# A two-layer recurrent/MoE kernel: expert inputs scattered to their slots, and the recurrent states kept as rows in DRAM

## The chip, the core and the metric

The program runs on one core of one Trainium2 chip. The metric is the device time of one execution in microseconds; the lower, the better. The kernel before took 1542.63 us (median of 3 runs, 1536.48 to 1543.17).

Five engines work side by side, each on its own in-order list of instructions: TensorE (PE, with its weight loads shown apart as PEld), VectorE (DVE), ScalarE (ACT), GpSimd (POOL) and SyncE (SP), which here only issues DMAs. Plain DMAs are issued from SP's queue, indirect ones (rows picked by a list of indices in SBUF) from POOL's.

## What is computed

`x` has 4 sequences (batches b = 0..3) of 1024 tokens with 256 channels, in float32. Two layers, each of the form `x = x + s * silu(f)`, where `s` and `f` both start from the layer-normed `x`:

```
xn = layernorm(x)
s  = gru(xn)                       # layer 0: gated linear recurrence over the 1024 steps
g  = silu(moe0(xn))                # 16 experts, 4 of them per token, hidden width 128
x  = x + s * g
xn = layernorm(x)
s  = attention(xn)                 # layer 1: proj = cos(theta)*cos(xn), softmax(proj proj^T / 4) proj W_c^T + b_c
g  = silu(moe1(xn))                # shared expert of width 512 + 16 routed ones of width 64
x  = x + s * g
```

The router of layer 0 takes a sigmoid of 16 scores per token, keeps the best two of four groups of experts, then the best four experts, and weights their outputs by the normalised scores.

## The kernel before, in words

The Python program lists instructions in the order of the calls below; the framework then orders each engine's list itself, by readiness in its own model of time and with earlier calls first, and puts in the semaphore waits. So work of a later call may stand before that of an earlier one (in the trace the weight loads of L635 are issued ahead of the row stores of L216). Tiles with the same tag share a fixed number of buffers (`bufs`); a tile waits until one of them is free.

**Layer 0** treats the batches as two groups, (0,1) and (2,3), of 2048 tokens each. For a group:

- `prep0` (L619): loads x in halves of 512 tokens (`load_half`, L84, tag `x`, XB = 5 buffers), `norms` (L180) gives mean and variance, `norm_transposed` (L204) writes the normed rows (L212), stores them to DRAM as `rows_in` (L216) and transposes them on PE to `xnT`. `route` (L272) computes the scores (matmuls L283) and picks the experts on DVE. `places` (L329) gives each (token, choice) pair a slot: the slots of an expert fill tiles of 128, at most 80 tiles for a group. Then it builds, slot by slot, the **list** of which token sits there: 64 times (16 token tiles x 4 choices) POOL compares (`at`, L384), DVE compares (`who`, L386) and PE multiplies (L389).
- `gru` (L455): for each half and each 128 channels (four rounds per batch, 16 in all) four matmuls (L464), three ACT instructions (L473 to L475), four DVE ones (L476 to L480) and a scan along time (L482). The states `hT` stay in SBUF, channels on partitions (tag `big_a`, two buffers).
- `experts0` (L485): 40 pairs of slot tiles. Per pair, POOL fetches 2 x 128 token rows of `rows_in` by the list (L493), PE transposes them (L506), gate and up projections with the weights of that tile's expert (8 matmuls, L530), silu and product, transposes (L547), the down projection (L555), and one store to `rows_out` (L569).
- `gated0` (L584): per 128 tokens, POOL gathers the four expert rows of each token from `rows_out` (4 x L593), DVE weights and adds them (L599, L601), ACT takes silu of a half (L604), PE turns the states to rows (L611), DVE multiplies and adds (L613, L616), SP stores `x1` (L617).

The calls stand in this order (L631 to L644):

```
xnTs, *routed0 = prep0(0)          # then the weights w0 (L635)
hTs = [gru(t) for t in xnTs]
experts0(0, ...)
xnTs, *routed1 = prep0(1)
gated0(0, ...) for b = 0, 1
experts0(1, ...)
hTs = [gru(t) for t in xnTs]
gated0(1, ...) for b = 2, 3
```

**Layer 1** (L647 to L816) goes batch by batch: `prep1` (norm, cosine projection into tag `big_a`, values, routing), `attend` (scores L699, exp L707, sums L713), `ffn1` for each half (L442, L446, L768, L782). `prep1(b+1)` is called between the two halves of batch b.

Of the kernel before, what the change touches and what calls it, by code (L numbers as in the profile page):

```python
# [8 lines left out]
F32 = mybir.dt.float32  # L9
F16 = mybir.dt.float16  # L10
I32 = mybir.dt.int32
# [11 lines left out]
XB, RB, YB = 5, 3, 3  # L23
E, G = 16, 4
TOPK = 4
GROUPS0 = ((0, 1), (2, 3))
WE = 3 * D


def slot_tiles(n):  # L30


    most = n * TOPK // P + E - 1
    return most + most % 2
# [8 lines left out]
INV_2PI = 0.15915494309189535  # L43
MAGIC = 12582912.0
# [4 lines left out]
def two_layer_kernel(  # L49
# [97 lines left out]

    count1 = const.tile([P, P], F32, tag="count1", name="count1")
    nc.gpsimd.iota(count1, [[1, P]], base=1, channel_multiplier=0, allow_small_or_imprecise_dtypes=True)
# [4 lines left out]

    token = const.tile([P, NG], F32, tag="token", name="token")
    nc.gpsimd.iota(token, [[P, NG]], base=-NG * P // 2, channel_multiplier=1, allow_small_or_imprecise_dtypes=True)
# [4 lines left out]
    b2_sb = const.tile([P, 2 * KC], F32, tag="b2", name="b2_sb")  # L161
    nc.vector.tensor_scalar(b2_sb, bzh_sb, 2.0, None, ALU.mult)
# [41 lines left out]
    def norm_transposed(halves_, stat, keep=None):  # L204


        xnT = work.tile([P, KC, S], F32, tag="xnT", name="xnT", bufs=2)
        for q in range(NQ):
            xn = work.tile([P, NS, D], F32, tag="r", name="xn", bufs=RB)
            shift, rstd = stat[q]  # L210
            for s in range(NS):
                nc.scalar.activation(  # L212
                    xn[:, s, :], halves_[q][:, s, :], AF.Identity, bias=shift[:, s : s + 1], scale=rstd[:, s : s + 1]
                )
            if keep is not None:
                nc.sync.dma_start(  # L216
                    out=keep.rearrange("(c p) d -> p c d", p=P)[:, q * NS : (q + 1) * NS, :], in_=xn
                )
# [110 lines left out]
    def places(em, g):  # L329
# [32 lines left out]
        nc.vector.tensor_scalar(base, base, float(P), 1.0, ALU.mult, ALU.add)  # L362
# [10 lines left out]
        ptile = small.tile([P, nt, TOPK], F32, tag="ptile", name="ptile", bufs=1)  # L373
        nc.vector.tensor_scalar(ptile, top[:, :, 0:TOPK], 1.0 / P, -0.5 - 0.5 / P, ALU.mult, ALU.add)
        nc.vector.tensor_scalar(ptile, ptile, MAGIC, None, ALU.add)
        nc.vector.tensor_scalar(ptile, ptile, MAGIC, None, ALU.subtract)
        pin = small.tile([P, nt, TOPK], F32, tag="pin", name="pin", bufs=1)
        nc.vector.scalar_tensor_tensor(pin, ptile, -float(P), top[:, :, 0:TOPK], ALU.mult, ALU.add)  # L378

        lst = bank("tp", 2)  # L380
        for c in range(nt):
            for k in range(TOPK):
                at = small.tile([P, P], F16, tag="at", name="at", bufs=4)
                nc.gpsimd.tensor_scalar(at, count1, pin[:, c, k : k + 1], None, ALU.is_equal)  # L384
                who = small.tile([P, ns], F16, tag="who", name="who", bufs=4)
                nc.vector.tensor_scalar(  # L386
                    who, count0[:, 0:ns], ptile[:, c, k : k + 1], token[:, c : c + 1], ALU.is_equal, ALU.mult
                )
                nc.tensor.matmul(  # L389
                    lst[:, 0:ns],  # L390
                    lhsT=at,
                    rhs=who,
                    start=(c == 0 and k == 0),
                    stop=(c == nt - 1 and k == TOPK - 1),
                )
        who_in = small.tile([P, ns], I32, tag=f"who_in{g}", name="who_in", bufs=1)
        nc.vector.tensor_scalar(who_in, lst[:, 0:ns], float(NG * P // 2), None, ALU.add)


        nc.vector.tensor_scalar(who_in, who_in, float(nt * P - 1), None, ALU.min)  # L400
        slot = small.tile([P, nt, TOPK], I32, tag=f"slot_i{g}", name="slot_i", bufs=1)
        nc.vector.tensor_scalar(slot, top[:, :, 0:TOPK], -1.0, None, ALU.add)
# [3 lines left out]
        for t in range(0, ns, 32):  # L406
            n = min(32, ns - t)
            done = small.tile([1, n, E], F32, tag="hit", name="done", bufs=1)
# [8 lines left out]
        return who_in, slot, top, pos, of_tile  # L417

    def weights_by_slot(comb, top, pos, g):
# [3 lines left out]
        for i in range(0, nt, NT):  # L423
            ts = slice(i, i + NT)
            shape = [P, NT, TOPK, E]
            hit = small.tile(shape, F32, tag="hit", name="hit", bufs=1)
# [10 lines left out]
    def gate_up(wg, wu, xr):  # L437
# [11 lines left out]

    rows_in = [nc.dram_tensor(f"rows_in{g}", (len(s) * S, D), F32).ap() for g, s in enumerate(GROUPS0)]  # L450
    rows_out = [
        nc.dram_tensor(f"rows_out{g}", (slot_tiles(len(s) * S) * P, D), F32).ap() for g, s in enumerate(GROUPS0)
    ]

    def gru(xnT):  # L455

        hT = work.tile([P, KC, S], F32, tag="big_a", name="hT", bufs=2)
        for q in range(NQ):
            cols = slice(q * TB, (q + 1) * TB)
            for c in range(KC):  # L460
# [10 lines left out]
                w = work.tile([P, 4, TB], F32, tag="big_b", name="gru")  # L471
                tz, co, tg, rl = (w[:, i, :] for i in range(4))
                nc.scalar.activation(tz, pk, AF.Tanh, bias=hb_sb[:, c : c + 1], scale=0.5)  # L473
                nc.scalar.activation(tg, pp, AF.Tanh, bias=hb_sb[:, KC + c : KC + c + 1], scale=0.5)
                nc.scalar.activation(rl, pp, AF.Relu, bias=b2_sb[:, KC + c : KC + c + 1], scale=2.0)  # L475
# [6 lines left out]
                nc.vector.tensor_tensor_scan(hT[:, c, cols], co, tg, before, ALU.mult, ALU.add)  # L482
        return hT

    def experts0(g, who_in, of_tile):  # L485

        ns = who_in.shape[1]
        offsets = {}
# [387 lines left out]
```

## Time and profile before

| | |
|---|---|
| median of 3 runs | 1542.63 us |
| the profiled execution | 1543.79 us |
| its span, first to last instruction | 1542.1 us |
| busy in it: PE / DVE / POOL / ACT | 1290.4 / 562.3 / 374.3 / 351.8 us |
| mean granted TensorE clock | 0.892 |
| DMA moved | 100.93 MB |

The profiled execution's time is its span and 1.7 us around it. Busy time is the sum of an engine's instructions; it is an average over stages with different limits. By the first and last instructions of each stage in the trace, the span divides like this:

| from to (us) | stage | length |
|---|---|---|
| 0 to 121 | load, norms, routing and the list of group 0; GRU of batches 0, 1 | 121 |
| 121 to 268 | experts of group 0 | 147 |
| 268 to 405 | routing and list of group 1, gather and gate of group 0 | 137 |
| 405 to 553 | experts of group 1 (with a rest of the gating of group 0) | 148 |
| 553 to 660 | GRU of batches 2, 3, gather and gate of group 1 | 107 |
| 660 to 685 | what is left of `prep1(0)` | 25 |
| 685 to 1542 | attention and feed-forward of layer 1 | 857 |

### The profile page before, as it was taken

Reading aid. Unit: us, or ns where it says so; the run is one execution under the profiler, and the core shown is the slowest. Engines: PE = TensorE matmul, PEld = TensorE weight load, DVE = VectorE, ACT = ScalarE, POOL = GpSimd, SP = SyncE. Lnnn points to the kernel's source line nnn. Section 1 sums busy time; section 2 is a strip of 40 time slices with the busy share of each in tenths; the row PEclk is TensorE's granted clock in tenths of the full one; section 3 lists DMA queues with packets and bytes.
Section 4 is the critical chain, followed back from the end, with each engine's and each line's share of the span. In section 5 each row is a group of like instructions: output and inputs, shape, how many; then the busy total and the mean of one; then the engine's idle time right before and its main releaser. Section 6 shows DMA issues by size and latency. Waiting matters only on the chain.

```text
span 1542.1 us, 13292 instructions
## 1 busy us (share of the span) xinstructions
PE 1290.4 (84%) x4424; PEld 753.4 (49%) x4424; DVE 562.3 (36%) x1438; ACT 351.8 (23%) x651; POOL 374.3 (24%) x437
## 2 busy tenths in 40 slices
PE   4836999713499971089999999999999999999998
PEld 3315888401278840056535356345365353564443
DVE  3882333367633364471226221144211244102212
ACT  4303333200133330052103132022121030221110
POOL 1096552589855437500000000000000000000000
PEclk9856999655599995579999999999999999999999
DMA  8105555323355754320001000010000000000000
GB/s 311 55 1 163 164 163 132 109 82 97 113 149 164 150 203 143 123 69 14 1 0 55 0 28 0 0 41 14 0 14 0 0 14 1 14 1 0 0 14 14
DMA packets 67666, 100.93 MB, mean 65 GB/s; under 512 B 7824, under 2 KB 57104, under 8 KB 66704
## 3 DMA queue, kind: packets, MB, share of 16 engines
q1 hardware_dynamic: 53776, 62.32, 11.9%
q0 software_dynamic: 13824, 37.77, 9.6%
q8 instruction: 37, 0.61, 0.2%
q14 instruction: 29, 0.24, 0.1%
HBM read 66.51 MB, written 33.55 MB: 65 GB/s over the span
## 4 chain that ended last, share of the span: by engine, by line
PE 75%; POOL 7%; DVE 6%; issue 5%; DMA 3%; another core or an unknown queue 3%; ACT 0%; SPq 0%; POOLq 0%; DVEq 0%; ACTq 0%
PE mm L442 11%; PE acc L782 11%; PE gu L442 11%; PE gu L530 9%; PE mm L699 7%; PE acc L713 7%; PE acc L555 4%; PE tp L768 4%; POOL r L593 4%; POOL at L384 3%; PE tp L506 2%; PE tp L675 2%; PE tp L283 2%; DMA r<-rows_out,slot_i 1%
## 5 line engine op out<-in xcount | busy, mean ns | idle before, releaser
L446 DVE TENSOR_TENSOR act<-sg,gu 128x512 f32<-128x512 f32 x96 | 65.8, 686 | 375.6 <-PE gu L442 358.4
L442 PE MATMUL mm<-xnT,w_sb 128*128 128x512 f32 x384 | 186.5, 609 | 0.0
L782 PE MATMUL acc<-act,w_sb 128*128 128x512 f32 x384 | 185.2, 607 | 0.0
L442 PE MATMUL gu<-xnT,w_sb 128*128 128x512 f32 x384 | 183.1, 598 | 0.0
L493 POOL DMA_INDIRECT xs<-rows_in,who_in x160 | 154.6, 966 | 104.9 <-PE tp L506 68.7
L530 PE MATMUL gu<-w_sb,xT 128*128 x640 | 157.6, 391 | 0.6 <-issue 0.5
L593 POOL DMA_INDIRECT r<-rows_out,slot_i x128 | 128.7, 1006 | 95.6 <-issue 31.5
L444 ACT ACTIVATE sg<-mm 128x512 f32<-128x512 f32 x96 | 57.2, 596 | 405.2 <-PE mm L442 391.6
L530 PEld LDWEIGHTS gu<-w_sb,xT 128*128 128x128 f32 x640 | 119.8, 197 | 15.7 <-issue 1.7
L699 PE MATMUL mm<-projT 128*128 128x512 f32 x256 | 122.4, 604 | 0.0
L713 PE MATMUL acc<-val,es 128*128 128x256 f32 x512 | 119.7, 379 | 0.0
L442 PEld LDWEIGHTS mm<-xnT,w_sb 128*128 128x128 f32 x384 | 67.2, 189 | 103.4 <-issue 102.0
L442 PEld LDWEIGHTS gu<-xnT,w_sb 128*128 128x128 f32 x384 | 73.1, 193 | 90.4 <-issue 90.4
L782 PEld LDWEIGHTS acc<-act,w_sb 128*128 128x128 f32 x384 | 72.8, 193 | 90.8 <-issue 83.7
L713 PEld LDWEIGHTS acc<-val,es 128*128 128x128 f32 x512 | 97.0, 190 | 35.8 <-issue 25.1
L389 PE MATMUL tp<-who,at 128*128 128x80 f16 x128 | 31.6, 248 | 97.0 <-POOL at L384 56.4
L384 POOL TENSOR_SCALAR at<-count,pin 128x128 f16<-128x128 f32 x128 | 86.5, 695 | 70.8 <-DVE pin L378 69.5
L549 DVE COPY hT<-tp 128x256 f32<-128x256 f32 x80 | 33.9, 424 | 169.1 <-PE tp L547 141.1
L555 PE MATMUL acc<-w_sb,hT 128*128 x320 | 83.3, 383 | 0.0
L464 PE MATMUL mm<-xnT,wzh_sb 128*128 128x512 f32 x128 | 68.7, 686 | 14.1 <-ACT gru L475 11.0
L768 PE MATMUL tp<-combT,sel 16*128 16x512 f32 x128 | 71.7, 640 | 0.0
L389 PEld LDWEIGHTS <-at 128*128 128x128 f16 x128 | 13.4, 105 | 117.6 <-POOL at L384 94.9
(174 smaller groups left out, 1355.2 us busy)
## 6 DMA issues: line engine op xcount, KB each, us to landing
rows_out<-o SPq DMA_DIRECT2D x80, 256.0 KB
x_half<-in_x_dram SPq DMA_DIRECT2D x16, 512.0 KB
x_half<-x SPq DMA_DIRECT2D x16, 512.0 KB
w_sb<-in_w_dram SPq DMA_DIRECT2D x4, 1536.0 KB
rows_in<-xn SPq DMA_DIRECT2D x8, 512.0 KB
x<-x_half SPq DMA_DIRECT2D x8, 512.0 KB
out_dram<-x_half SPq DMA_DIRECT2D x8, 512.0 KB
xs<-rows_in,who_in POOLq DMA_INDIRECT x160
```

The source lines that it names most:

```text
L384: nc.gpsimd.tensor_scalar(at, count1, pin[:, c, k : k + 1], None, ALU.is_equal)
L442: nc.tensor.matmul(ps, lhsT=w[:, kc, :], rhs=xr[:, kc, :], start=(kc == 0), stop=(kc == KC - 1))
L446: nc.vector.tensor_tensor(h, sg, u, ALU.mult)
L464: nc.tensor.matmul(ps, lhsT=wzh_sb[:, kc, c0 : c0 + P], rhs=xnT[:, kc, cols], start=(kc == 0), stop=(kc == KC - 1),)
L493: nc.gpsimd.indirect_dma_start(out=xs[:, i, :], out_offset=None, in_=rows_in[g], in_offset=bass.IndirectOffsetOnAxis(ap=who_in[:, 2 * j + ...
L530: nc.tensor.matmul(ps[:, i * D : (i + 1) * D], lhsT=xT[:, i, kc, :], rhs=w0_sb[:, bass.ds(off + kc * D, D)], start=(kc == 0), stop=(kc == ...
L555: nc.tensor.matmul(ps[:, i * D : (i + 1) * D], lhsT=hT[:, i, :], rhs=w0_sb[:, bass.ds(offset(2 * j + i) + 2 * D, D)], start=True, stop=True,)
L593: nc.gpsimd.indirect_dma_start(out=r[:, k, :], out_offset=None, in_=rows_out[g], in_offset=bass.IndirectOffsetOnAxis(ap=slot[:, c, k : k + ...
L699: nc.tensor.matmul(ps, lhsT=projT[:, kc, t * P : (t + 1) * P], rhs=projT[:, kc, cols], start=(kc == 0), stop=(kc == KC - 1),)
L713: nc.tensor.matmul(av[s // 2][:, (s % 2) * D : (s % 2 + 1) * D], lhsT=es[:, s * P : (s + 1) * P], rhs=val[:, t, :], start=(t == 0 and s % ...
L768: nc.tensor.matmul(wide, lhsT=sel[:, j].rearrange("k h i -> k (h i)"), rhs=combT, start=True, stop=True,)
L782: nc.tensor.matmul(yT[kc], lhsT=w[:, kc * P : (kc + 1) * P], rhs=h, start=(j == 0), stop=(j == NCH - 1))
```

## The change

1. **No list, no gather of inputs.** `places` no longer builds `who_in`. It computes for each (token, choice) a DRAM row (`row`), and a new function `dispatch` scatters the normed rows straight from SBUF to `rows_in`, which now has one row for each slot: 64 indirect DMAs from POOL for each group. `experts0` then loads its inputs with plain DMAs, four slot tiles at a time (`QUAD`), and stores its outputs four at a time. The slots of four tiles are interleaved so that a partition's four rows lie together.
2. **Zeros.** Slots that no token fills would be undefined, so both `rows_in` are first filled with zeros, from one zeroed SBUF tile (tag `big_a`).
3. **Order.** Both groups' `prep0`, with its dispatch, and all four `gru` come first, then `experts0(0)`, `gated0(0)`, `experts0(1)`, `gated0(1)`.
4. **States as rows.** `gru` turns its states to rows at once (the same PE transposes, an ACT copy) and stores them to `hidden_rows`; `gated0` loads them again and needs no PE.
5. **Smaller edits.** Norms are written in place into the x tile (XB = 8 buffers instead of 5), and taken for each batch instead of each group. The GRU's four DVE instructions besides the scan become two, and its three ACT instructions four. In `gated0` the first product moves from DVE to ACT, and silu is built from a tanh. The expert inputs share the tag `r` (3 buffers) with the gathered rows; the expert outputs, the state rows and both tiles of `gated0` share the tag `y` (3 buffers), as attention's result does.

The slot tiles of a group stay 80 (79 rounded up to a multiple of four instead of two).

```diff
-XB, RB, YB = 5, 3, 3
+XB, RB, YB = 8, 3, 3
...
-            xn = work.tile([P, NS, D], F32, tag="r", name="xn", bufs=RB)
+            xn = halves_[q]
...
-        lst = bank("tp", 2)
-        for c in range(nt):
-            for k in range(TOPK):
-                at = small.tile([P, P], F16, tag="at", name="at", bufs=4)
-                nc.gpsimd.tensor_scalar(at, count1, pin[:, c, k : k + 1], None, ALU.is_equal)
...
+        mark = top[:, :, 0:TOPK]
+        rest = small.tile([P, nt, TOPK], F32, tag="ptile", name="ptile", bufs=1)
+        nc.vector.tensor_scalar(rest, mark, 1.0 / P, MAGIC, ALU.mult, ALU.add)
...
+        nc.vector.scalar_tensor_tensor(row, quad, QUAD * P - 1.0 - QUAD * MARK, rest, ALU.add, ALU.add)
...
-                w = work.tile([P, 4, TB], F32, tag="big_b", name="gru")
-                tz, co, tg, rl = (w[:, i, :] for i in range(4))
-                nc.scalar.activation(tz, pk, AF.Tanh, bias=hb_sb[:, c : c + 1], scale=0.5)
+                w = work.tile([P, 3, TB], F32, tag="gru", name="gru", bufs=2)
+                co, tg, v1 = (w[:, i, :] for i in range(3))
+                nc.scalar.activation(co, pk, AF.Tanh, bias=hb_sb[:, c : c + 1], scale=0.5)
                 nc.scalar.activation(tg, pp, AF.Tanh, bias=hb_sb[:, KC + c : KC + c + 1], scale=0.5)
...
+                nc.scalar.activation(v1, pp, AF.Identity, bias=b21_sb[:, KC + c : KC + c + 1], scale=2.0)
+                nc.scalar.activation(co, co, AF.Identity, bias=half, scale=-0.5)
+                nc.vector.scalar_tensor_tensor(tg, tg, 1.0, v1, ALU.add, ALU.max)
+                nc.vector.scalar_tensor_tensor(tg, co, 1.0, tg, ALU.subtract, ALU.mult)
...
+            hr = work.tile([P, NS, D], F32, tag="y", name="hr", bufs=YB)
...
+                nc.scalar.copy(hr[:, s0 : s0 + 2, :].rearrange("p s d -> p (s d)"), tp)
+            nc.sync.dma_start(out=halves(hidden_rows, b)[:, q * NS : (q + 1) * NS, :], in_=hr)
+
+    def dispatch(g, tokens, row):
+
+        n = len(tokens) * NS * TOPK
+        views = dram_disjoint_views(rows_in[g], n)
+        for i in range(n):
+            c, k = divmod(i, TOPK)
+            nc.gpsimd.indirect_dma_start(
+                out=views[i],
+                out_offset=bass.IndirectOffsetOnAxis(ap=row[:, c, k : k + 1], axis=0),
+                in_=tokens[c // NS][:, c % NS, :],
+                in_offset=None,
+            )
...
+            if j % per == 0:
+                xs = work.tile([P, QUAD, D], F32, tag="r", name="xs", bufs=RB)
+                nc.sync.dma_start(out=xs, in_=by_quads(rows_in[g])[j // per])
...
+            if j % per == per - 1:
+                nc.sync.dma_start(out=by_quads(rows_out[g])[j // per], in_=o)
...
+            hr = load_half(hidden_rows, b, q)
...
-                nc.vector.tensor_scalar(y[:, s, :], r[:, 0, :], w[:, c, 0:1], None, ALU.mult)
+                nc.scalar.activation(y[:, s, :], r[:, 0, :], AF.Identity, scale=w[:, c, 0:1])
...
+            t = work.tile([P, NS, D], F32, tag="y", name="t", bufs=YB)
+            nc.scalar.activation(t, y, AF.Tanh, scale=0.5)
+            nc.vector.scalar_tensor_tensor(y, t, 1.0, y, ALU.add, ALU.mult)
+            nc.vector.scalar_tensor_tensor(y, y, -0.25, hr, ALU.mult, ALU.mult)
+            nc.vector.tensor_tensor(xs, xs, y, ALU.add)
...
+        row, top, pos, of_tile = places(em, g)
+        dispatch(g, [t for b in GROUPS0[g] for t in hs[b]], row)
...
+    zeros = work.tile([P, 2 * S], F32, tag="big_a", name="zeros", bufs=2)
+    nc.gpsimd.memset(zeros, 0.0)
+    for g, rows in enumerate(rows_in):
+        a = rows.rearrange("(p n) d -> p (n d)", p=P).rearrange("p (m z) -> p m z", z=2 * S)
+        nc.sync.dma_start(out=a, in_=zeros.unsqueeze(1).to_broadcast(a.shape))
+    routed = []
...
+    for g in range(len(GROUPS0)):
+        routed.append(prep0(g))
+        if g == 0:
...
+                nc.sync.dma_start(out=w0_sb[:, cols], in_=w0[:, cols])
+        for b, xnT in zip(GROUPS0[g], routed[g][0]):
+            gru(xnT, b)
+    for g, bs in enumerate(GROUPS0):
+        _, row, w, of_tile = routed[g]
+        experts0(g, of_tile)
+        for i, b in enumerate(bs):
+            gated0(g, i, b, row, w)
```

`dram_disjoint_views`, a function of the framework, gives 64 views of the same DRAM rows that are declared not to overlap each other; the loads of `rows_in` depend on all of them.

## The prediction

> **What bounds the kernel now.** First the page's busy times and its 40 slices, to see whether one engine fills the span.
>
> ```profile
> PE 1290.4 (84%) x4424; PEld 753.4 (49%) x4424; DVE 562.3 (36%) x1438; ACT 351.8 (23%) x651; POOL 374.3 (24%) x437
> ...
> PE   4836999713499971089999999999999999999998
> ...
> POOL 1096552589855437500000000000000000000000
> PEclk9856999655599995579999999999999999999999
> ```
>
> A slice is 38.6 us. From slice 18 on (layer 1) PE is full; all PE idle time lies in layer 0, where POOL is busy instead. Next the busy times by stage (columns: stretch, length, then PE, PEld, DVE, ACT, POOL, granted clock, DMA share, GB/s).
>
> ```profile
> 75.00:121.00 46.00, 15.84 (x64) 6.63 (x64) 36.90 (x114) 3.13 (x4) 44.73 (x64) 0.51 0.00 1
> 121.00:145.00 24.00, 15.00 (x52) 11.07 (x53) 3.78 (x14) 10.70 (x21) 15.35 (x16) 0.64 0.47 140
> 145.00:262.00 117.00, 117.00 (x642) 102.08 (x641) 38.69 (x88) 43.54 (x90) 60.51 (x64) 0.99 0.61 169
> ...
> 302.00:405.00 103.00, 31.64 (x110) 15.66 (x111) 66.13 (x219) 6.87 (x8) 86.56 (x108) 0.53 0.28 87
> ...
> 430.00:550.00 120.00, 118.93 (x647) 103.62 (x648) 40.58 (x93) 44.59 (x92) 60.51 (x64) 0.99 0.57 152
> ...
> 585.00:660.00 75.00, 8.37 (x32) 6.08 (x32) 36.20 (x90) 10.26 (x14) 46.65 (x48) 0.50 0.42 128
> ...
> 685.00:1542.00 857.00, 850.14 (x2377) 420.98 (x2376) 229.03 (x518) 166.65 (x316) 0.00 (x0) 0.99 0.03 10
> ```
>
> Experts (145-262, 430-550) and layer 1 are bound by PE at full clock; the list (75-121) and the stretches 302-405 and 585-660 by POOL, with PE idle for 30, 71 and 67 us. Third, which POOL work that is: the groups by line (busy, mean ns, idle before).
>
> ```profile
> L493 POOL DMA_INDIRECT xs<-rows_in,who_in x160 | 154.6, 966 | 104.9 <-PE tp L506 68.7 <-issue 28.6 <-remote 4.9
> L593 POOL DMA_INDIRECT r<-rows_out,slot_i x128 | 128.7, 1006 | 95.6 <-issue 31.5 <-DVE gru L476 29.0 <-PE tp L222 23.0
> L384 POOL TENSOR_SCALAR at<-count,pin 128x128 f16<-128x128 f32 x128 | 86.5, 695 | 70.8 <-DVE pin L378 69.5 <-DVE who L386 0.9
> ```
>
> Each indirect DMA holds POOL for 0.95 us, and the timeline starts the next 1.25 us after the last (0.30 us lies between). The list paces L384 at 0.58 to 0.7 us. So layer 0 alternates: POOL's list or gathers with PE idle, then PE's experts.
>
> **What the skill says.** "TensorE: Matmul & The Clock Gate", section "What's actually happening": the array runs at half clock after an idle window of about 3.4 us. The trace agrees: clock 0.50 to 0.53 in the idle stretches, 0.99 in the experts, and a 512-column matmul of L464 takes 592 ns at the median, 1221 at most. "DMA: Bandwidth & Descriptors", section "Issuing engines are not separate DMA queues": transfers from SP and POOL run on the same engines and interleave; at 134-136 us the trace has both queues at work and the engines full. Same page, "Two DMAs through the same engine are not ordered": only the completion semaphore tells that data has landed; so each load of `rows_in` must wait for all 64 scatters of its group. Same page, "Where 436 GB/s comes from": about 358 GB/s between HBM and one core; the trace moved 356 GB/s at 10-40 us, with the engines 97% taken.
>
> **The change part by part.** The sum is made against the profiled execution (1543.79 us, a span of 1542.1 and 1.7 around it; the runs' median is 1.2 below it). Before is 121 + 147 + 137 + 148 + 107 + 25 + 857 = 1542.
>
> *List removed.* 2 x 64 rounds of L384, L386, L389: the first 45 us lie on the path (74.6 to 119.7), the second inside 302-405. The row numbers cost DVE seven small instructions of about 0.2 us instead of seven: nothing.
>
> *Dispatch added.* 64 scatters per group, on the path for group 0. The trace has no scatter. Nearest row: a gather of the same 128 x 1 KB, 1.25 us apart. Bounds: 0.95 (no gap between two) and 3.04 + 0.95 = 4.0 us (each waits until the one before has landed; the first fetch was issued at 121.1 and PE read it at 124.14, 3.04 us). Since the views are disjoint I take 1.25: 64 x 1.25 = 80 us. First scatter: the numbers behind L384 were ready at 74.2. The GRU's DVE work in the way shrinks from 3.44 us a round (0.42 + 0.41 + 0.685 + 0.68 + 1.24) to 2.61 (2 x 0.685 + 1.24), five rounds stood before 74: -4. So 70, and dispatch ends at 150. Then 3 us landing, about 4 to load the first 512 KB (the first x half took 4.8 from issue at 5.03 to use at 9.86), 4 to fill the pipeline: **experts run at 161** (before: 145).
>
> *Experts.* 80 pairs x 3.25 us (the period of L530 from 149.8 to 260.3) = **260 us**, back to back: group 1's routing and its 80 us dispatch (150-230) lie under group 0's experts (161-291), with 60 us to spare. The gathers of group 0 (64 x 1.25 = 80) stand on POOL behind both dispatches and start at 294, under group 1's experts (291-421). The plain loads replace 160 x L493, which was hidden already: no gain in the steady state, but the slow starts 121-145 and 405-430 fall away. I keep **8 us** for such stalls (the unnamed waits there are 7.4 and 6.0 us) and **3** for passing from one group to the next.
>
> *GRU and routing of group 1* move ahead. They need x(2,3), which SP may have queued behind the zeros: see below. GRU of a batch is bound by ACT: four rounds x (4 x 0.69) = 11 us, and four copies of 0.59 for the rows. Most runs in 62-161, where PE has nothing else; I let **12 us** of PE work spill into the experts. A new wait: the first load of `rows_in` holds SP until dispatch 0 has landed. Row stores of batches 2, 3 queued behind it would keep their `y` buffers, and with three of those the GRU would stop until 153; then 27 us of PE work (its 64 matmuls at 0.43) spill, 15 more. The two stretches 302-405 and 553-660 vanish, but for these 12.
>
> *Zeros added.* 2 x 80 x 128 rows x 1 KB = 21 MB. At 356 GB/s 59 us; the trace shows no pure store stream, so from 21/0.49 = 43 (the fastest slice of 545-585 moved 492 GB/s) to 21/0.178 = 118 us (half rate). SP issues x(0,1) at 5.03, before POOL's memset can be done: POOL's setup ended at 5.1, and 2048 columns at about 0.92 ns (945 ns for 1024, L115) take 1.9. So zeros run from 12: group 0's half ends at 42 (at half rate at 71, about when scattering begins), both at 71, then w0 (6 MB, 18 us) and x(2,3) (2 MB, 6 us) by about 100. w0 is needed at 161. Row numbers of group 1 then take some 55 us as in the first pass (16 to 74): 155. Cost on the path: nothing, covered by dispatch 0; without this cover, that is were the zeros ahead of x(0,1), about 55 us. On SP the row stores and w0 stand behind the zeros; nobody waits for those before 161.
>
> *Gate.* `gated0` leaves PE. For b = 0 it needs 32 gathers: 294 + 40 + 5 = 339, so `prep1(0)` can run under the experts; its PE work is **16 us** (670.9 to 685 and two transposes). It could not before: both `big_a` buffers held states until 640. `gated0(1)` (421 to about 506) lies under attention of batch 0; its result is first needed by `prep1(2)`, over 300 us later. ACT gets 32 x 0.59 more, 19 us, DVE gives 12 back: neither is near its limit. *Layer 1* stays **857**.
>
> Sum: 161 + 260 + 8 + 3 + 12 + 16 + 857 = 1317, with 1.7 around it **1319 us**.
>
> **Rivals.** *Late start* (18%): the zeros go ahead of x(0,1), or their stores crawl, or the engines wait during the dispatch. For it: the framework orders by its own model of time, and waits of 15 us without a known releaser stood beside streaks of gathers (286 to 301). Against it: x loads are ready first. 1319 + 55 = 1374.
>
> *Cover fails at the hand-over* (14%): `gated0(1)` and attention contend for the three `y` buffers (y and t against two of attention), or instructions waiting for gathered rows stand in DVE's list ahead of the experts' copies. PE, queued behind, then waits. Layer 1 held until 421 + 80 + 10 = 511 instead of 437: +74, 1393.
>
> *Scatters one at a time* (7%, the slower side): each waits for the last. With period s > 2.2 us the second dispatch, not the experts, sets the time: 70 + 128 s + 7 + 130 + 16 + 857 = 1080 + 128 s. It equals 1542 at **s = 3.6 us**; at 4.0 it gives 1592. For it: the store's landing isn't in the trace. Against: gathers run 1.25 apart without waiting, and the views are made to free them.
>
> *No effect* (3%): the order comes out as before, since the framework sorts by readiness, 1543. Against it: the buffers and the data flow differ.
>
> **How the numbers follow.** Forecast 58%: 1319. Its own range goes from 1287 (scatters at 0.95, -19; no stalls, -8; GRU spill of 7, -5) to 1345 (half-rate zeros delay x(2,3) by 59 us, of which about 25 come to the path; or the 15 of the GRU's stop and 10 more of stalls). Late start and hand-over, 32% together, go from there to 1405, with 10 us more of stalls on the latter. Scatters one at a time and no effect, 10%, are left out, so the range is 1285 to 1405. About 0.5% (8 us) is what a measurement can tell from no change. Faster: 0.58 + 0.18 + 0.14 = 0.90; same 0.03; slower 0.07.
>
> **What would show it.** Right: first scatter near 70, the last near 150, 1.25 us apart; PE busy over 95% from 165 on, with no idle stretch of 50 us; gathers under the second experts; the first scores (L699's) near 440. PE's busy sum falls by the list's 32 us and by cold matmuls, to about 1240. Wrong: scatters over 2 us apart, x(0,1) landing after 60 us, PE waiting for `y` buffers after 421, or experts slower than 3.25 us a pair beside the gathers.

## The result, and the profile after

| | before | after |
|---|---|---|
| median, us (4 runs each) | 1541.18 | 1638.30 |
| span of the profiled execution, us | 1542.1 | 1635.9 |

After to before is 1.0645, with a 95% interval of 1.0605 to 1.0684: the change makes the kernel slower by 97 us. The forecast was 1319 us. In the experiments below the kernel before, run beside them, takes either 1541 to 1547 us (on three chips) or 1517 to 1520 us (on two others); every result is given with that time, and only runs of one level are compared with each other.

The page of the kernel after: busy times, then PE, POOL and the granted clock in 40 slices of 40.9 us.

```profile
PE 1260.1 (77%) x4296; PEld 741.7 (45%) x4296; DVE 514.3 (31%) x1252; ACT 385.6 (24%) x716; POOL 262.6 (16%) x277
...
PE   5731861599403999003999999999999999999998
...
POOL 1176057200374000672000000000000000000000
PEclk9865785799755999556999999999999999999999
```

PE's busy sum fell by 30 us and POOL's by 112, as intended, yet the span grew by 94. Where POOL has a 6 or 7 (counting from 0: slices 2, 3 and 6 with scatters, 11, 16 and 17 with gathers), PE has 0 to 3. Before, POOL's fetches for the experts lay beside a full PE (slices 4, 5 and 11 to 13); now none of POOL's work lies beside a full PE.

Busy time by stage of the kernel after (stretch, length, then PE, PEld, DVE, ACT, POOL, clock, DMA share, GB/s):

```profile
110.00:166.00 56.00, 9.87 (x23) 4.75 (x21) 1.21 (x4) 5.50 (x9) 36.67 (x39) 0.59 0.35 124
...
226.00:300.00 74.00, 20.65 (x78) 15.62 (x77) 2.02 (x5) 6.33 (x11) 54.92 (x58) 0.59 0.41 146
300.00:427.00 127.00, 118.37 (x642) 102.70 (x642) 42.00 (x95) 44.19 (x91) 0.00 (x0) 0.96 0.45 146
430.00:513.00 83.00, 0.00 (x0) 0.00 (x0) 30.60 (x54) 10.96 (x19) 63.78 (x64) 0.50 0.50 154
513.00:652.00 139.00, 134.50 (x720) 116.37 (x720) 48.44 (x105) 49.67 (x101) 0.50 (x1) 0.96 0.49 160
660.00:747.00 87.00, 0.00 (x0) 0.00 (x0) 33.41 (x69) 12.03 (x21) 64.08 (x63) 0.50 0.55 175
790.00:1636.00 846.00, 839.13 (x2358) 416.11 (x2356) 219.40 (x459) 155.32 (x298) 0.00 (x0) 0.99 0.03 9
```

In the two dispatches (110-166 and 226-300) the engines other than POOL mostly stand still (PE works 18% and 28% of the time), at a DMA share of 0.35 to 0.41: neither compute nor bytes are the limit. In the two gather stretches (430-513 and 660-747) PE does nothing at all, and its clock is at 0.50. The experts alone (300-427, 513-652) and layer 1 (from 790) run as before.

The groups by line show that the parts themselves came out as priced:

```profile
L479 POOL DMA_INDIRECT rows_in<-x_half,row x128 | 127.2, 993 | 164.5 <-issue 90.6
L593 POOL DMA_INDIRECT r<-rows_out,row x128 | 129.5, 1012 | 320.7 <-issue 320.0
```

A scatter costs POOL what a gather does (0.99 and 1.01 us), and the timeline has the next 1.26 us after the last: the first at 75.4, the 64th at 157.3.

**Where the forecast lost 319 us** (1638 to 1319). It had group 0's experts end at 291 and group 1's at 444; they end at 427 and 652. So 136 us are lost by the end of group 0's experts, 225 - 153 = 72 at group 1's, and after 652 come 984 us where 16 + 857 were forecast: 111.

### The profile page after: what moved, and what is told of

Read it like the earlier page. It is cut to its first block, busy times and chain, and to the rows that moved or that the text cites. A ratio compares the mean times of both kernels' runs of the same rounds, so it can differ in the third digit from the quotient of the medians.

```text
span 1635.9 us, 12646 instructions
## 1 busy us (share of the span) xinstructions
PE 1260.1 (77%) x4296; PEld 741.7 (45%) x4296; DVE 514.3 (31%) x1252; ACT 385.6 (24%) x716; POOL 262.6 (16%) x277
## 4 chain that ended last, share of the span: by engine, by line
PE 72%; DVE 8%; another core or an unknown queue 6%; issue 6%; DMA 3%; POOL 2%; ACT 2%; SPq 0%; ACTq 0%; DVEq 0%; POOLq 0%
PE mm L418 11%; PE acc L777 10%; PE gu L418 10%; PE gu L528 9%; PE acc L708 7%; PE mm L694 7%; PE acc L553 4%; PE tp L763 4%; PE tp L277 3%; POOL r L593 2%; PE tp L502 2%; PE tp L670 2%; DMA r<-rows_out,row 1%; DVE y L601 1%
## 5 line engine op out<-in xcount | busy, mean ns | idle before, releaser
L593 POOL DMA_INDIRECT r<-rows_out,row x128 | 129.5, 1012 | 320.7 <-issue 320.0
L528 PE MATMUL gu<-w_sb,xT 128*128 x640 | 157.3, 390 | 3.8 <-ACT xT L506 3.8
L216 PE MATMUL tp<-ident,x_half 128*128 128x128 f32 x128 | 25.6, 351 | 167.7 <-ACT x_half L210 139.4
L479 POOL DMA_INDIRECT rows_in<-x_half,row x128 | 127.2, 993 | 164.5 <-issue 90.6
L502 PE MATMUL tp<-ident,xs 128*128 128x128 f32 x320 | 51.5, 288 | 109.9 <-DMA xs<-rows_in 88.2
L216 PEld LDWEIGHTS tp<-ident,x_half 128*128 128x128 f32 x128 | 18.7, 178 | 182.6 <-ACT x_half L210 127.1
L502 PEld LDWEIGHTS tp<-ident,xs 128*128 128x128 f32 x320 | 42.3, 149 | 119.4 <-DMA xs<-rows_in 88.6
```

The lines of the kernel that those rows point to most:

```text
L479: nc.gpsimd.indirect_dma_start(out=views[i], out_offset=bass.IndirectOffsetOnAxis(ap=row[:, c, k : k + 1], axis=0), in_=tokens[c // NS][:, ...
L502: nc.tensor.transpose(tp[:, at : at + P], xs[:, j % per * 2 + i, kc * P : (kc + 1) * P], ident)
L528: nc.tensor.matmul(ps[:, i * D : (i + 1) * D], lhsT=xT[:, i, kc, :], rhs=w0_sb[:, bass.ds(off + kc * D, D)], start=(kc == 0), stop=(kc == ...
L593: nc.gpsimd.indirect_dma_start(out=r[:, k, :], out_offset=None, in_=rows_out[g], in_offset=bass.IndirectOffsetOnAxis(ap=row[:, c, k : k + ...
```

## Experiments

### The first loss: what stops the engines beside the dispatch?

The timeline of the kernel after, inside the first dispatch (start, length, engine, line, operation, and in brackets the idle time before it and what ended it; first PE, then DVE, then ACT):

```profile
110.51 1.06 PE L216 MATMUL tp<-ident,x_half 128*128 128x128 f32 x4
111.37 3.17 PE L444 MATMUL mm<-xnT,wzh_sb 128*128 128x512 f32 x6
134.49 2.07 PE L444 MATMUL mm<-xnT,wzh_sb 128*128 128x512 f32 x2 [19.95 <-issue]
```

```profile
123.24 0.69 DVE L218 COPY xnT<-tp 128x512 f32<-128x512 f32 x1 [13.49 <-remote]
...
166.01 0.69 DVE L218 COPY xnT<-tp 128x512 f32<-128x512 f32 x1 [41.50 <-remote]
```

```profile
128.84 0.58 ACT L220 COPY xnT<-tp 128x512 f32<-128x512 f32 x1 [19.73 <-remote]
129.44 1.28 ACT L453 ACT_TABLE_LOAD   x1
133.75 0.69 ACT L453 ACTIVATE gru<-mm,hb_sb 128x512 f32<-128x512 f32 x1 [3.02 <-remote]
...
166.05 0.58 ACT L220 COPY xnT<-tp 128x512 f32<-128x512 f32 x1 [28.67 <-remote]
```

DVE's L218 and ACT's L220 wait for PE's transposes alone. The profile has PE done with those by 111.6, and yet DVE sets out at 123.2 and ACT at 128.8. In the other direction a hand-over is prompt: ACT's L453 ends at 134.44 and PE starts at 134.49. So what PE finishes is seen late, or PE finishes late (its ends are modelled).

The trace also records when PE's semaphore, the counter on which the others wait, changes. From 20 to 75 us each change follows the end of a matmul by 0.015 us. In the dispatch, the changes for work that ends from 110.7 to 112.8 come at 118.3, 123.2, 128.8 and 133.7, and those for four ends from 139.1 to 139.8 at 165.92, 165.95, 165.98 and 166.03. In e12_after_third, an experiment below in which no signal is late, four such changes lie 0.1 to 0.4 us apart (from 111.8 to 112.6, from 118.1 to 118.5), not 0.03. So at least these four were done earlier, and their signals were held up and let go together; DVE and ACT set out within 0.1 us of them. "PE's signals are late" means this below. What holds them up no run here shows.

The last waits end at 166, 8 us after the last scatter. The kernel before had one long wait of this kind behind PE, beside a streak of gathers: its `sc` stood until 301.0, 25 us, behind matmuls that the profile ends at 286.2, and there too three changes of PE's semaphore came together, from 301.01 to 301.11.

The first four experiments took the dispatch and the buffers apart.

**e1_pause_short** and **e2_pause_long** put a copy after each scatter (256 or 768 columns):

```diff
                 in_offset=None,
             )
+            pad = small.tile([P, 256], I32, tag="pad", name="pad", bufs=1)
+            nc.gpsimd.tensor_copy(pad, row[:, c, k : k + 1].to_broadcast([P, 256]))
```

> Each scatter is followed by a copy of 256 columns on POOL (some 0.3 us), so that scatters stand about 1.6 us apart instead of 1.26. Theory 1 (a gapless streak of indirect DMAs on POOL holds up what the other engines wait for): the waits of 13 to 41 us of PE, ACT and DVE inside the first dispatch (110 to 166 us) and inside the second (226 to 298) go; the row numbers of group 1 come by 160 instead of 214.7, the first dispatch ends near 180, the experts of group 0 run from about 186 to 320 instead of 226 to 427; the whole takes about 1530. Rival (the stalls come from bytes on the DMA engines, or from the order of the instructions, whatever POOL's spacing): the waits stay, and the two dispatches are 22 us longer each: 1660 to 1685.

> The same with a copy of 768 columns (some 0.8 us): scatters about 2.1 us apart. Theory 1: no waits of over 5 us without a cause in either dispatch; the first dispatch takes 134 us (to about 210), the second as long beside the experts of group 0 (216 to 350); about 1560, so slower than the short pause if that is enough, faster than it if 1.6 us is still too dense. Rival: the waits stay and both dispatches are longer by 54 us: 1690 to 1740.

**e3_half_rows** halves the bytes and keeps the number:

```diff
-    rows_in = [... (slot_tiles(len(s) * S) * P, D), F32) ...]
+    rows_in = [... (slot_tiles(len(s) * S) * P, P), F32) ...]
-                in_=tokens[c // NS][:, c % NS, :],
+                in_=tokens[c // NS][:, c % NS, 0:P],
-                nc.sync.dma_start(out=xs, in_=by_quads(rows_in[g])[j // per])
+                for h in range(2):
+                    nc.sync.dma_start(out=xs[:, :, h * P : (h + 1) * P], in_=by_quads(rows_in[g])[j // per])
```

> The scatters move only the first 128 columns of each row (512 B instead of 1 KB) into slots of half the width, and the experts load these into both halves of their tile: it leaves out the second half of each row. As many scatters[...], half the bytes; the zero fill is halved too. Theory 1 (POOL's streak, not the bytes): scatters still 1.26 us apart, the waits of PE, ACT and DVE in both dispatches stay within some 10 us of what they were, the experts of group 0 end at 427 give or take 10, and the whole takes 1625 to 1650. Rival (bytes on the DMA engines hold the others up): the waits shrink by half or more, the experts of group 0 end by 370: under 1590.

**e4_own_xs** gives the experts' rows buffers of their own:

```diff
-XB, RB, YB = 8, 3, 3
+XB, RB, YB = 6, 3, 3
-                xs = work.tile([P, QUAD, D], F32, tag="r", name="xs", bufs=RB)
+                xs = work.tile([P, QUAD, D], F32, tag="xs", name="xs", bufs=2)
```

> The experts' rows get a tile name of their own (two buffers) instead of sharing three with the gathered rows of the gate; to make room x gets 6 buffers instead of 8. Theory 1: the experts of group 1 no longer wait 88 us for their rows: the loads are issued near 430 instead of 510, and the tiles start at about 433 beside the gathers of group 0. As these gathers are a streak too, the experts crawl until it ends near 513, as those of group 0 did from 226 to 298 (about a quarter of their work in 72 us): a gain of 15 to 40, 1600 to 1623. If the gathers don't hold them up, a gain of some 80: 1558. Rival (the order of the instructions keeps the experts behind the gathers, not the buffers): PE stays idle from 427 to 513, and the time stays within 10 us of 1638.

Measured: 1586.5, 1614.3, 1568.0 and 1575.0, beside a kernel before of 1519.5. Against 1638 all four look like gains. They aren't: **e12_after_third**, the unaltered kernel beside a before of 1517.2, takes 1564.0. At that level the pauses cost 23 and 50 us, half rows and own buffers gain nothing (+4, +11; single runs). And the late signals of PE are in none of these traces. The four say nothing on them, and the expectations, all made against 1638, are void in that part.

> The changed kernel unaltered, as the yardstick of this call. With before at about 1541: 1638 to 1645 and the waits behind PE in both dispatches. With before at about 1520: if those waits are the chip's, they are missing here too, and the experts of group 0 advance in 20 us steps in the second dispatch alone, as in e4_own_xs: some 1590 to 1610.

Its mechanism was right, missing waits and steps of 20 us; its time was too high by 26 us at least (1564 for 1590 to 1610). The change is thus slower than the kernel before at this level as well, by 47 us. What the traces of this level do show is a second cause, which the first had covered. In e12_after_third the first dispatch runs beside PE at 53 us of work in 74; group 0's experts start at 184 and still take until 354. SP's list there (start, length, operation):

```profile
189.64 0.47 SPq L495 DMA_DIRECT2D xs<-rows_in  x1
208.83 0.36 SPq L89 DMA_DIRECT2D x_half<-hidden_rows  x1
209.29 0.45 SPq L495 DMA_DIRECT2D xs<-rows_in  x1
229.09 0.38 SPq L89 DMA_DIRECT2D x_half<-in_x_dram  x1
229.58 0.45 SPq L495 DMA_DIRECT2D xs<-rows_in  x1
```

Each load of the experts' rows (L495) stands behind a load for the gate (L89). The gate's load goes into an `x` buffer that holds tokens of group 1, and must wait until all 16 scatters of that tile have landed: 16 x 1.26 = 20 us a step. One quad, 6.5 us of PE work, is fed per step.

**e5_after_again** and **e6_gate_loads_pool** were taken together, beside a before of 1540.9. The second issues the gate's loads on POOL:

```diff
-            xs = load_half(x, b, q)
-            hr = load_half(hidden_rows, b, q)
+            xs = load_half(x, b, q, nc.gpsimd)
+            hr = load_half(hidden_rows, b, q, nc.gpsimd)
```

> The changed kernel once more, unaltered, as the yardstick for its neighbours, since all times of this chip lie lower. Theory 1 (the streak itself holds the engines up, whenever it runs): the waits without a named releaser stand between 110 and 166 us again, of the same length, and the experts of group 0 run from 226 to 427. Theory 2 (two separate causes: an occasional hold-up in the first dispatch, and in the second SP's list, in which the gate's loads of x and hidden rows stand between the experts' loads and each wait for a tile of tokens to be scattered, 16 x 1.26 = 20 us): the first may be there or not, the second must be: the experts of group 0 advance in steps of 20 us until the second dispatch ends. About 1.065 times the time of before on this chip if the first is there, 1.04 if not.

> The sixteen loads of x and of the hidden rows that the gate makes are issued on POOL, whose own list the scatters and gathers stand in, instead of on SP; nothing else. Theory 2: in the second dispatch no load of the experts' rows stands behind a wait for scatters any more; the experts of group 0 take about 130 us from their start instead of 201, beside the same scatters 1.26 us apart; 65 to 75 us less than the unaltered kernel beside it. Theory 1 (the streak holds up the engines): the steps of 20 us stay, and the time within 10 us of the unaltered one.

1641.0 and 1638.9. At this level the late signals are there each time (DVE's L218 waits 45.7 us in the one, 45.0 in the other), and they hide SP's list: theory 2's gain of 65 to 75 did not come. What they depend on is told by the next six; beside five of them the kernel before takes 1543 to 1547.

> The changed kernel with a copy of 256 columns on POOL after each scatter, as in e1_pause_short. There the kernel before took 1519.5 us, 21 less than beside e5 to e8, and none of the waits without a named releaser showed; so that run may speak of its chip and not of the pause. If the dense streak delays PE's signals (theory 1, narrowed: only PE's, and only where the kernel before takes about 1541), then with before at about 1541 the waits behind PE of 10 to 45 us in the first dispatch go with the pause: the experts of group 0 end by 330 to 350 instead of 427 (second dispatch still in steps from SP's list), 1545 to 1575. If the spacing is not what matters, they stay: 1660 to 1690. With before at about 1520 it says nothing new: 1586.

1591.1 beside 1517.2: the other level again, nothing new.

> e6_gate_loads_pool (the gate's loads on POOL, nothing else) with a copy of 256 columns on POOL after each scatter. With before at about 1520: the steps of 20 to 25 us that e9_pause_short_again has in the second dispatch are gone, since no load of the experts' rows stands behind a wait for scatters: 40 to 60 less than its 1591. With before at about 1541: if the spacing frees PE's signals, the waits behind PE go in both dispatches and the experts of group 0 end near 330 to 350 instead of 427: 1545 to 1565, against 1639 for e6; if it doesn't, 1660 to 1690.

1555.8 beside 1543.5, within the expected span: 83 less than e6 at the nearest level, though each dispatch is longer. The stages of e14_loads_pause, against the first two rows of the kernel after:

```profile
110.00:166.00 56.00, 49.66 (x167) 28.89 (x167) 37.12 (x105) 28.90 (x46) 50.58 (x63) 0.83 0.21 76
...
205.00:338.00 133.00, 132.92 (x720) 115.48 (x720) 43.32 (x99) 50.37 (x102) 80.01 (x116) 0.98 0.66 221
```

PE works 50 us of the first 56 instead of 10, and group 0's experts run without a gap beside the second dispatch, with more bytes moving (221 GB/s) than in the stalled one (146). The scatters stand 1.56 us apart at the median (1.77 on average in the first dispatch, with its breaks). The pauses, which add some 0.3 us to each of 2 x 64 scatters, pay for themselves. The experts of group 0 end at 338, where 291 was forecast; 44 of these last 47 us lie in their later start (205 for 161).

> e6_gate_loads_pool with scatters of half rows (the second 128 columns of each row are left out, the experts load the first half twice), 1.26 us apart as before. With before at about 1541: if it is the number and density of the indirect DMAs that delays PE's signals, the waits behind PE stay: 1625 to 1650, as e6's 1639; if it is their bytes, they shrink: under 1600. With before at about 1520: no waits behind PE either way; the gate's loads on POOL alone remove the steps of 20 us that e3_half_rows had: 1568 less 30 to 60.

1653.0: at 1.26 us apart half the bytes don't help (PE works 0.7 us from 120 to 150), nor do half as many 4 KB packets of POOL's queue, about 1060 for 2110 in e6 from 74 to 162 us. The bytes of the scatters are out as the cause of the late signals.

> As e14_loads_pause, with the copy after every fourth scatter only (1.26 us apart within four, 1.34 on average). With before at about 1541: if a break now and then is enough for PE's signals, the waits behind PE go and the shorter dispatches (86 us instead of 100) give 1535 to 1555; if the mean rate must fall towards 1.6 us, most of the waits stay: 1600 to 1640. With before at about 1520: 1525 to 1545.

The edit leaves the copy out for `k < TOPK - 1`. 1633.2: DVE's L218 and the experts' L551 still wait up to 19 and 31 us. A short break after every fourth scatter isn't enough; the scatters then stood 1.37 to 1.40 us apart on average. Whether it is the wider spacing that helps, or some work of POOL's own after each scatter, these runs don't separate: every pause was such a copy.

> The changed kernel with the copy of 256 columns after each scatter, the gate's loads on SP as in the original: e14_loads_pause without its other edit. With before at about 1541: no waits behind PE, but steps of 25 us (16 x 1.56) in the second dispatch, since SP's list holds the experts' loads behind the gate's: some 30 to 40 more than e14's 1556, so 1585 to 1600. If the pause did all of it, 1550 to 1565. With before at about 1520: 1586 to 1592 again.

1597.0 beside 1547.1: SP's list alone, with PE's signals prompt, costs 1597 - 1556 = 41 us (37 when 3.6 is taken off for the slower kernel before). Its list has the steps of 25 us:

```profile
215.17 0.37 SPq L89 DMA_DIRECT2D x_half<-in_x_dram  x1
...
240.13 0.37 SPq L89 DMA_DIRECT2D x_half<-hidden_rows  x1
...
265.08 0.38 SPq L89 DMA_DIRECT2D x_half<-in_x_dram  x1
...
290.62 0.37 SPq L89 DMA_DIRECT2D x_half<-hidden_rows  x1
```

> e6_gate_loads_pool once more. With before at about 1520, where PE's signals are not late: without the steps in the second dispatch the experts of group 0 take about 130 us from 184, to 315 to 325 instead of 354: 1525 to 1535 against 1564 for the unaltered kernel there. With before at about 1541: 1639 again.

1649.9 beside 1547.1: as e6, the gate's loads alone gain nothing at this level. So the first loss has two causes that cover each other: curing SP's list alone gains 2 or less, the pause alone some 44, both 83 to 85 (single runs; four runs of one kernel differed by 8). All waits of PE, its weight loads, ACT and DVE without a named releaser between 75 and 340 us, added up over the engines:

| before beside it | scatters apart, us | kernels | sum of these waits, us |
|---|---|---|---|
| 1541-1547 | 1.26 | after, e5, e6, e7, e8, e17, e15 (half bytes) | 244 to 274 |
| 1547 | 1.37 to 1.40 on average | e18 | 203 |
| 1543-1547 | 1.56 | e13, e14, e16 | 0 |
| 1517-1520 | 1.26 to 1.98 | e1, e2, e3, e4, e9 to e12 | 0 |

The spacing is the median but for e18. By this count the kernel before has 43 us itself in its profiled run.

### The second loss: group 1's experts and the gathers

In the kernel after, PE waits 88 us in one piece for group 1's first rows:

```profile
PE tp L502 <- DMA xs<-rows_in: 88.2, 1, 88.2
```

Their load was issued at 510 only: SP's list has it behind the gate's loads of group 0 until 500, and then `xs` waits for one of the three `r` buffers, which it shares with the gate's gathered tiles; these are written earlier in the program. e4_own_xs removed the sharing: its experts start at 383, do 30 us of work in the first 92 beside the gathers and end at 584, where e12_after_third's end at 579. No gain. The wait for buffers is real, but once it is gone the same time is lost in DVE's and ACT's lists, where instructions that wait for gathered rows stand ahead of the experts' copies. Waits of e4_own_xs from 385 to 480 (total, times, longest):

```profile
ACT y L599 <- DMA r<-rows_out,row: 55.1, 14, 5.9
DVE y L601 <- DMA r<-rows_out,row: 38.7, 25, 4.5
PE tp L545 <- DVE h L539: 34.5, 3, 16.7
...
PE acc L553 <- DVE o L565: 21.4, 1, 21.4
```

**e7_interleave** adds to e6, among the edits named below, that the gate's steps are written between the experts' pairs and need no `y` buffers:

```diff
+            if j >= 2 and j % 2 == 0:
+                next(steps, None)
...
-                nc.scalar.activation(y[:, s, :], r[:, 0, :], AF.Identity, scale=w[:, c, 0:1])
+                y = r[:, 0, :]
+                nc.scalar.activation(y, y, AF.Identity, scale=w[:, c, 0:1])
...
+                nc.scalar.activation(y, y, AF.Silu)
+                nc.vector.scalar_tensor_tensor(y, y, -0.5, hr[:, s, :], ALU.mult, ALU.mult)
+                nc.vector.tensor_tensor(xs[:, s, :], xs[:, s, :], y, ALU.add)
...
+                yield
```

> As the last; further the experts' rows have two buffers of their own (x 7, and one buffer for the helper tile of the routing), the gate works in place in the gathered tile, 128 tokens at a time, with one Silu instead of Tanh and its two steps, and so needs no y buffers, and its sixteen steps for group 0 are written between the pairs of group 1's experts, one per two pairs. Theory 2: experts and gathers then run together: group 1's experts follow group 0's at once and take 130 to 140 us, and the whole saves a further 75 to 85 us. The gathers of group 1 still hold layer 1 up by 80 to 100 us. Theory 1: the streak of gathers holds up the experts: they take 200 us or more, and the saving is under 40.

1588.9 beside 1540.9, 50 less than e6, not 75 to 85: between 438 and 540 PE works 66 us of 102 beside the gathers. Part of the stretch stays lost, and the 50 us belong to all its edits together.

### The third loss: layer 1 and the gathers of group 1

PE waits 104.8 us in one piece for `x_half` of layer 1, until 756.7. The first load of `x1` leaves SP at 689 only. The gate's own loads were all issued by 528, but they hold the `x` buffers, and the gathers free these one by one (SP's waits of the kernel after from 660 to 790):

```profile
SPq L89 <- DVE y L601: 56.1, 2, 33.9
SPq L89 <- DVE y L608: 27.7, 2, 15.0
```

In the other 68 us, from 689 to 757, the norms of batch 0 stand in DVE's and ACT's lists among gate instructions that wait for gathered rows (36 us of such waits on ACT, 15 on DVE). On DVE the norms run from 701.8 to 754.3, in short pieces such as these:

```profile
722.92 0.75 DVE L186 BATCH_NORM_STATS2 stats<-x_half 128x6 f32<-128x256 f32 x2
...
733.18 0.17 DVE L189 TENSOR_SCALAR va<-mv 128x8 f32<-128x8 f32 x1 [2.62 <-remote]
...
748.99 0.20 DVE L192 RECIPROCAL rstd<-rstd 128x8 f32<-128x8 f32 x1
```

L189 reads what DVE's own L187 left at 730.56, and still waits 2.62 us: beside the gathers of this level DVE's signals come late too, by 3 us at most, so it isn't PE alone.

**e8_interleave_both** puts group 1's gate steps between the chunks of `ffn1` of batch 0:

```diff
             last = (j, h)
+            next(steps, None)
         down(*last)
         gT = []
```

> As the last, and the sixteen gate steps of group 1 are written between the chunks of the layer-1 experts of batch 0, so that its first stage needs nothing from them. Theory 2: no idle stretch of PE of over 20 us is left after group 0's experts start; a further 75 to 95 us, some 1310 to 1350 in all, faster than both kernels. Theory 1: layer 1's first batch is slower by the gathers' 80 us, and the saving under 30.

1537.7 beside 1540.9: a further 51. The two dispatches still stall here (L548 waits 44.8 us in the second), so 1310 to 1350 was out of reach at this level; that expectation left the late signals out.

### All causes together

**e10_both_pause_short** and **e11_both_pause_scatter** add pauses to e8; **e13_spaced_both** pauses after the scatters only, starts the steps at pair 8 and stores the GRU's rows from ACT:

```diff
-            nc.sync.dma_start(out=halves(hidden_rows, b)[:, q * NS : (q + 1) * NS, :], in_=hr)
+            nc.scalar.dma_start(out=halves(hidden_rows, b)[:, q * NS : (q + 1) * NS, :], in_=hr)
-            if j >= 2 and j % 2 == 0:
+            if j >= 8 and j % 2 == 0:
```

> e8_interleave_both with a copy of 256 columns on POOL after each scatter and each gather. Theory 1, narrowed: group 1's routing and GRU run beside the first dispatch, the experts of group 0 start near 185 and take 130 to 140 us; group 1's the same beside the gathers: the whole 1320 to 1380. If the spacing doesn't matter: 40 to 60 us slower than e8_interleave_both's 1538, about 1590.

> The same with 448 columns after each scatter (about 1.9 us apart), and none after the gathers. If 1.56 us apart is still too dense for PE's signals, this one is the faster of the two by the dispatches' part; if 1.56 is enough, it is slower by the longer first dispatch (64 x 0.3 = 20 us) and by what the unspaced gathers hold up (20 to 40 us): 1360 to 1430.

> e8_interleave_both with a copy of 256 columns on POOL after each scatter, the gate's steps for group 0 starting six pairs later (at pair 8), and the stores of the GRU's rows issued on ACT, which writes them, instead of SP, where the first load of the experts' rows stands ahead of them. With before at about 1520 (as beside e9 to e12): 10 to 40 less than e11_both_pause_scatter: 1390 to 1425. With before at about 1541: if the spacing frees PE's signals, 1400 to 1450, faster than e8_interleave_both by 90 to 140; if it doesn't, 1540 to 1580.

1438.7 and 1433.9 beside 1517.2, both slower than expected. As no signal is late at that level, they don't tell whether spaced gathers would help at the other. e13: 1441.7 (4 runs) beside 1543.5 (7 runs), **0.934 of the kernel before, interval 0.932 to 0.937**, faster than both kernels. Its 96 us less than e8 belong to its three edits together. Its stages:

```profile
197.00:340.00 143.00, 142.38 (x778) 124.12 (x779) 45.13 (x103) 53.06 (x107) 90.89 (x131) 0.98 0.71 235
340.00:440.00 100.00, 61.33 (x256) 49.61 (x255) 49.62 (x133) 29.69 (x71) 64.03 (x65) 0.83 0.64 204
440.00:510.00 70.00, 70.00 (x389) 61.08 (x388) 25.61 (x62) 31.77 (x65) 1.57 (x2) 1.00 0.53 173
510.00:580.00 70.00, 44.56 (x148) 29.11 (x147) 36.49 (x107) 24.19 (x41) 33.95 (x33) 0.68 0.52 177
```

Of the 123 us that it stays above the forecast, 36 lie in the later start of the experts (197 for 161: the scatters stand 1.79 us apart on average for 1.25), 39 in PE's idle time beside the gathers of group 0 and 25 at the start of layer 1; the rest was not placed. Its gathers have no pauses, and beside them late signals of PE come back: after 340 us ACT and DVE have 42 us of such waits.

## Why the prediction was wrong, point by point

- *List removed, dispatch added*: right. First scatter at 75 for 70, 1.26 us apart for 1.25, the last of group 0 at 157.3 for 150. Scatters one at a time, the rival on the slower side, did not happen: the kernel got slower by another mechanism than the one named.
- *Zeros*: right on their place, and cheaper than taken. Zeros and `w0` together moved 428 GB/s from 19 to 75 us, where I took 356. So the limit of about 358 that the prediction cites did not hold here, and the trace before had shown it already: 397 GB/s from 555 to 565 us. `x(0,1)` came first, and `x(2,3)` was there from 96 to 102.
- *Experts of 3.25 us a pair and layer 1 of 857*: right where nothing runs beside them.
- ***"Group 1's routing and its 80 us dispatch lie under group 0's experts"***, and group 1's preparation under the first dispatch: this step failed (136 us). Overlap was read from busy times. The late start rival (18%) named the engines waiting during the dispatch and the sign seen in the profile before, 286 to 301, and I priced it at 55 us once; it comes in both dispatches. The runs show in its place late signals, which vanish with a pause after each scatter (e14 against e6, 83 us), but neither with half the bytes (e15) nor with a pause after every fourth (e18), and SP's list beneath them (41 us, e16 against e14). Why the signals are late stays open. The prediction saw that SP stands at the first load of `rows_in`; it did not ask which loads SP would place between the experts'.
- ***"The gathers of group 0 start at 294, under group 1's experts"***: failed (72). SP's list and shared `r` buffers block the start (trace), and without the sharing DVE's and ACT's order loses it as well (e4). The hand-over rival (14%) had the second half, for the later hand-over.
- ***"`gated0(1)` lies under attention of batch 0"***: failed (111, e8 got 51 back). Shared `x` buffers hold the loads of `x1` until 689, and the order of DVE's and ACT's lists the norms until 757.
- *The chances*: 90% for faster came from adding rivals as separate cases of +55 and +74. All overlaps depend on the same thing, that POOL's streaks run beside other work, and the profile before had no dense streak beside which PE was fully busy. Its experts had two gathers per 3.25 us; the streaks of 1.25 us stood in exactly the stretches where PE was idle.

## What to carry to other kernels

Before counting on work lying beside a stream of DMAs, walk each in-order list (SP, DVE, ACT) and each shared buffer name across the overlap: one load that waits for another stage's buffer, or one instruction that waits for gathered data, stops all that stands behind it. A cover that the profile shows at one density (two gathers in 3.25 us) is no evidence for a denser streak. And a fix that gains nothing may be hidden by a second cause: here the gate's loads on POOL gained 2 us alone, the pauses 44, both together 85.

## What the hardware showed that was not expected

- Beside scatters 1.26 us apart, signals of PE were held up in every trace at the level of 1541 to 1547: waits of up to 50 us, and a signal up to 36 us after the end that the trace gives for PE (e6: 130.3 and 166.1). With a pause after each scatter (1.56 us apart at the median) there were none beside the scatters, and at the level of 1517 to 1520 none even at 1.26. What differs between the two levels, which came on different chips, stays open; so does whether such waits are the 22 us or so by which the kernel before itself differs.
- A copy of 256 columns on POOL after each scatter, 0.4 us of work that is of no use, went with a kernel 44 us faster at one level (1641 to 1597) and 23 slower at the other (1564 to 1587).
- Stores of one zeroed tile and loads of `w0` ran at 428 GB/s together, against 356 for the loads at 10 to 40 us of the kernel before.
